# Head 2 turned by VectorE in tiles 1 to 6, and sums moved behind head 3's scores

## The chip, the core and the metric

The kernel runs on one core of a Trainium2 chip. The core has five engines that run their own instruction streams: TensorE (PE in the profile; its weight loads are PEld), VectorE (DVE), ScalarE (ACT), GpSimd (POOL) and SyncE (SP), which only issues transfers. Sixteen transfer (DMA) engines move data that SP and POOL ask for. The metric is the device time in microseconds (us) of one execution, as a median of runs; lower is better.

## The reference

The input x has 16 batches of 1024 nodes with 256 features; adj is a 1024 x 1024 matrix of 0 and 1 per batch. Two layers follow, each added to x:

```python
h = relu(layernorm(x))                          # layer 0
Q, K, V = h @ W.T + b, in 8 heads of 32         # Wq, Wk, Wv
s = where(adj == 0, -inf, Q @ K.T / sqrt(32))   # 1024 x 1024 for each head
x = x + (softmax(s) @ V, heads joined) @ Wo.T + bo

h = relu(layernorm(x))                          # layer 1
e = leaky_relu((h * a_0) @ h.T, 0.2)            # where adj == 1; other kinds have a_1 to a_3
x = x + softmax(where(adj == 1, e, -9e15)) @ h
```

The data has no kinds above 1, so a generic path at the kernel's end is skipped.

## The kernel before

A batch is cut into 8 tiles of 128 rows (t = 0 to 7), 128 tiles in all. The main loop goes over tiles s, and inside over the 8 heads h. Three stages overlap in it, all written out in one order by hand (`tc.manual_schedule()`), so each engine works off its instructions in program order:

- `now`: layer 0 of tile s (class `Attend`). `scores` (L461) puts a head's 128 x 1024 scores into one of two PSUM places (`sides`); heads 4 and 6 use side 1, the others side 0. `softmax_max` (L473, DVE) masks them and takes the maximum, writing the tile `p`; `softmax_exp` (L490, ACT) makes the exponentials, one head later.
- `was`: what is left of the tile before: the sums of heads 4 to 7 (`combine(1)`, L526, PE), their scaling (`combined`, L536, DVE), the output product (L541) and the residual (L547).
- `edge` and `edge_was`: layer 1 of the tiles 9 and 10 places earlier (class `Edges`). Its scores use side 1 (L633, L627), its maximum is L656, its own blocks come at h == 0, and `gather(0)` and `gather(1)` (L698, PE) multiply its probabilities with h, half of the columns each.

`piece` and `piece_was` project queries, keys and values of a batch that comes later.

The sums need each head's probabilities turned, with the keys along the partitions. There are two ways, two heads after the scores:

- `turn`: PE transposes eight 128 x 128 squares into PSUM (L590), and ACT copies them out in two halves (L591).
- `turn_blocks` and `place_blocks`: DVE transposes 32 x 32 blocks (L381), and SP issues four transfers of 128 KB (L386) that put the blocks in their places in the tile `pT`. The keys then come out in another order, which the values match for the heads in `MIXED`.

`by_blocks(t)` says which heads go the second way: 0, 1, 4 and 5 in tiles 1 to 6, 0, 1 and 4 in tile 7, 4 and 5 in tile 0. Layer 1's blocks go the second way in all tiles of the loop. Where a head's way doesn't fit its key order (`MIXED`), `softmax_exp` writes into a second tile `p` in the other order; before, that is heads 0 and 1 of tile 0 and head 5 of tile 7.

Around the change, the order in a tile is, at h == 3: scores of head 3, layer 1's maximum, head 3's maximum, exponential of head 2, layer 1's mirror copy (L647), value bias (L355), blocks of head 1, the next tile's query load (`load_queries`, L428, SP). At h == 4, with `late_scores`: exponential of head 3, `turn` of head 2, scores and maximum of head 4, and then `block()`: `combine(1)`, `combined`, `gather(0)`. At h == 7 come `gather(1)`, the store, and `combine(0)`, the sums of heads 0 to 3.

SP's queue in a tile, in order: layer 1's blocks, head 0's, head 1's, the query load, head 4's blocks, the write of x1 (L552), head 5's blocks, the store (L708).

Of the kernel before, what the change touches and what calls it, by code (L numbers as in the profile page):

```python
# [26 lines left out]
MIXED = (0, 1, 4, 5)  # L27
BY_BLOCKS = {7: (0, 1, 4), 0: (4, 5)}


def by_blocks(t):
    return BY_BLOCKS.get(t, MIXED)


def place_of(h):
# [12 lines left out]
def gnn_kernel(  # L48
# [308 lines left out]
    def load_key(b, h):  # L357
        kt = keys.tile([P, N], F32R, tag=f"k{h}", name=f"k{h}_{b}")
        c, r = divmod(h, GROUP)
        nc.sync.dma_start(  # L360
            out=kt.bitcast(F32),
            in_=kds[b][c, r * HD : (r + 1) * HD]
            .rearrange("d w n -> (d w) n").unsqueeze(1).to_broadcast([2 * HD, 2, N]),
        )
        keysets.setdefault(b, {})[h] = kt
# [410 lines left out]
    def attend_of(s):  # L776
        return Attend(*divmod(s, NT)) if 0 <= s < B * NT else None

    def edges_of(s):
        s -= LAG  # L780
        return Edges(*divmod(s, NT), s >= (B - 1) * NT) if 0 <= s < B * NT else None

    def piece_of(s):
        s += LEAD
        return Piece(*divmod(s, NT)) if s < B * NT else None

    with tc.manual_schedule():
        first = [Piece(0, 0, 4), Piece(0, 4, 4)]
        piece_was, piece_next = Piece(1, 0), piece_of(0)
        now, nxt = attend_of(0), attend_of(1)  # L790
# [48 lines left out]
        for s in range(B * NT + 1):  # L839
            b, t = divmod(s, NT)  # L840

            def load_keys(h, end):
                if t == NT - 1 and b + 1 < B and 2 * h + end in KEY_STEPS:
                    load_key(b + 1, KEY_STEPS.index(2 * h + end))
                if t == 0 and 0 < b < B and 2 * (HEADS + h) + end in KEY_STEPS:
                    load_key(b, KEY_STEPS.index(2 * (HEADS + h) + end))

            late_turn = None

            def block():  # L850
                if edge_was and not t:
                    edge_was.gather(0)
                if was:
                    was.combine(1)
                if not t and piece_was:
                    piece_was.biased()
                if was:
                    was.combined()
                if edge_was and t:
                    edge_was.gather(0)  # L860

            nxt2, edge_nxt, piece_nxt = attend_of(s + 2), edges_of(s + 1), piece_of(s + 1)
            for h in range(HEADS):
                ending, eh = (now, h - 1) if h >= 1 else (was, HEADS - 1)
                turning, th = (now, h - 2) if h >= 2 else (was, HEADS + h - 2)

                load_keys(h, 0)


                late_scores = h == 4 and now and 1 in by_blocks(t)  # L870
                if now and not late_scores:
                    now.scores(h)
                if h == 0 and piece_was:
                    piece_was.halve(0)
                if s == 0 and h == 1:
                    first[1].values()
                if h == 3 and edge:
                    edge.softmax_max()
                if h == 6:
                    if was:  # L880
                        was.residual()
                    norms(was, piece_nxt)
                if now and not late_scores:
                    now.softmax_max(h)
                if h == 4 and piece:
                    piece.normed()


                if h == 1 and edge:
                    edge.keep(0)  # L890
                if h == 2 and gone:
                    gone.turned_normed()
                if h == 5 and piece:
                    piece.turn()
                    piece.turned()
                if ending:
                    ending.softmax_exp(eh)

                if h == 3 and edge:
                    edge.keep(1)  # L900
                if h == 3 and was:
                    was.turned_reciprocals()
                if h == 3 and piece_was:
                    piece_was.raised(1)
                if h == 3 and edge:
                    edge.bend()


                if h == 3 and t and piece_was:
                    piece_was.biased()  # L910
                if h == 5 and was:
                    was.output()
                if h == 4 and not late_scores:
                    block()
                    late_turn = turning
                    load_keys(h, 1)
                    continue
                if h == 5 and late_turn:
                    late_turn.turn(2, 0)
                    late_turn.turn(2, 1)  # L920
                if h == 0 and t == 0 and was:
                    for half in range(2):
                        was.turn(HEADS - 3, half, nc.scalar.copy)
                if turning and th in by_blocks(turning.t):
                    turning.turn_blocks(th)
                    turning.place_blocks(th)
                elif turning and (h, t) != (HEADS - 1, NT - 1):
                    turning.turn(th, 0)
                    turning.turn(th, 1)
                if late_scores:  # L930
                    now.scores(h)
                    now.softmax_max(h)


                if h == 0:
                    if edge:
                        edge.score(0)
                    if gone:
                        gone.normed()
                    if edge_was:  # L940
                        edge_was.turn_blocks()
                        edge_was.place_blocks()
                if h == 1:
                    if gone:
                        gone.turn_normed()
                    if piece_was:
                        piece_was.project(1, 0)
                        piece_was.project(1, 1)
                    if was:
                        was.reciprocals()  # L950
                    if piece_nxt:
                        piece_nxt.load()
                if h == 2:
                    if edge:
                        edge.score(1)
                    if piece_was:
                        piece_was.values()
                    if was:
                        was.turn_reciprocals()
                        was.add_bias()  # L960
                if h == 3:
                    if nxt:
                        nxt.load_queries()
                    if edge:
                        edge.leak()
                    if piece_was:
                        piece_was.halve(1)
                    if edge_was:
                        edge_was.load_nodes()
                    if nxt:  # L970
                        nxt.flag()
                        nxt.mask()
                if h == 4:
                    block()
                if h == 5:
                    if piece_was:
                        piece_was.write_queries()
                    if edge_nxt:
                        edge_nxt.prepare()
                    if nxt2:  # L980
                        nxt2.load()
                if h == 6:
                    if piece:
                        piece.project(0, 0)
                        piece.project(0, 1)
                        piece.raised(0)
                    if edge:
                        edge.softmax_exp()
                    if was:
                        was.keep()  # L990
                    if now:
                        now.load_nodes()
                if h == 7:
                    if edge_was:
                        edge_was.gather(1)
                        edge_was.store()
                    if now:
                        now.combine(0)
                load_keys(h, 1)
            gone, was, now, nxt = was, now, nxt, nxt2  # L1000
            edge_was, edge = edge, edge_nxt
            piece_was, piece = piece, piece_nxt
# [84 lines left out]
```

## Time and profile before

| | |
|---|---|
| median of 3 runs | 3004.3 us (3004.06 to 3010.76) |
| the profiled execution's own time | 3006.89 us |
| its span, first to last instruction | 3005.0 us |
| granted TensorE clock | 0.998 |
| PE, DVE, ACT, POOL busy | 97%, 83%, 88%, 72% |
| mean DMA rate | 234 GB/s |

The busy share of PE is modelled from pipelined matmuls. In groups of instructions the columns after the count are the busy time in us, the mean of one in ns, and the idle time of the engine ahead of them with what ended it. Tiles are counted here from a tile's first softmax maximum to the next tile's.

### The profile page before, as it was taken

The numbers are of one execution on the slowest core, as the hardware profiler recorded it, in microseconds if no ns is written. First come the engines' busy times: TensorE is split into PE (matmuls) and PEld (weight loads), VectorE is DVE, ScalarE is ACT, GpSimd is POOL, SyncE is SP. The second block draws the span as 40 slices with busy tenths as digits, with TensorE's granted clock in tenths as the row PEclk, the third lists the DMA queues.
The fourth block names the chain that finished last, engine by engine and source line by source line (L and its number), as shares of the span: only waits on it lengthen the run. The fifth ranks groups of instructions, "written<-read, shape, count | busy, mean of one in ns | idle before, by whom it ended". The sixth has DMA issues, their size and how long they took to land. (4 is left out here: it accounts for less than half of the span.)

```text
span 3005.0 us, 95721 instructions
## 1 busy us (share of the span) xinstructions
PE 2903.3 (97%) x36594; PEld 2234.0 (74%) x36594; DVE 2495.4 (83%) x4405; ACT 2635.5 (88%) x5191; POOL 2171.0 (72%) x2999
## 2 busy tenths in 40 slices
PE   7889999999999999999999999999999999999998
PEld 5777777777777777777777777777777777777664
DVE  5888888888888888878888887888888888788875
ACT  5999989999898999999999998998989999898882
POOL 3767877777787777778778777777877777786542
PEclk9999999999999999999999999999999999999999
DMA  7787877778778887877878777787787878777763
GB/s 243 233 259 215 248 229 243 250 227 261 227 227 254 239 260 218 243 247 230 269 222 245 239 237 249 227 267 222 231 255 232 263 219 243 245 230 250 196 174 100
DMA packets 607041, 704.03 MB, mean 234 GB/s; under 512 B 64305, under 2 KB 537777, under 8 KB 606577
## 3 DMA queue, kind: packets, MB, share of 16 engines
q1 hardware_dynamic: 537504, 485.68, 54.4%
q0 software_dynamic: 66960, 210.04, 21.7%
q8 instruction: 294, 4.82, 0.7%
q10 hardware_dynamic: 2112, 2.10, 0.2%
q14 instruction: 171, 1.39, 0.1%
HBM read 252.98 MB, written 134.22 MB: 129 GB/s over the span
## 5 line engine op out<-in xcount | busy, mean ns | idle before, releaser
L473 DVE CUSTOM_DVE_ANT_0 p<-s,neg 128x1024 f32<-128x1024 f32 x1024 | 1238.6, 1210 | 344.8 <-PE s L461 324.6
L490 ACT ACTIVATE p<-p,nmx 128x1024 f32<-128x1024 f32 x1024 | 1236.4, 1214 | 51.6 <-DVE nmx L473 43.1
L461 PE MATMUL s<-k,qt 128*128 128x512 f32 x2048 | 743.2, 445 | 30.4 <-DMA k<-kd 8.3
L591 ACT COPY pT<-trp 128x512 f32<-128x512 f32 x1056 | 566.5, 593 | 77.5 <-PE trp L590 77.1
L590 PE MATMUL trp<-ident,p 128*128 128x128 f32 x4480 | 587.3, 274 | 27.4 <-ACT pT L591 15.0
L590 PEld LDWEIGHTS trp<-ident,p 128*128 128x128 f32 x4480 | 516.0, 140 | 118.9 <-ACT pT L591 30.2
L381 DVE STREAM_TRANSPOSE blocks<-p 128x1024 f32<-128x1024 f32 x472 | 585.2, 1240 | 11.1 <-ACT p L680 10.6
L526 PE MATMUL acc<-pT,v 128*32 128x128 f32 x16384 | 507.8, 273 | 9.3 <-ACT full L309 8.9
L526 PEld LDWEIGHTS acc<-pT,v 128*32 128x32 f32 x16384 | 453.4, 110 | 80.9 <-issue 36.1
L698 PE MATMUL acc<-h,pT 128*32 128x256 f32 x8192 | 510.0, 381 | 1.9 <-DMA pT<-blocks 1.6
L441 POOL TENSOR_SCALAR neg<-adj 128x1024 bf16<-128x1024 int32 x128 | 467.8, 3655 | 11.9 <-ACT neg L453 1.9
L676 POOL TENSOR_TENSOR sel<-sel,less 128x1024 f32<-128x1024 f32 x120 | 287.8, 2398 | 201.7 <-ACT less L665 201.7
L461 PEld LDWEIGHTS s<-k,qt 128*128 128x128 f32 x2048 | 312.4, 190 | 153.0 <-issue 82.5
L698 PEld LDWEIGHTS acc<-h,pT 128*32 128x32 f32 x8192 | 265.3, 110 | 190.7 <-issue 48.8
L633 PE MATMUL s<-h1T,ha 128*128 128x512 f32 (+2 forms) x744 | 272.8, 490 | 2.8 <-ACT h1T L569 2.8
L490 ACT ACTIVATION_READ_ACCUMULATOR p<-p,nmx 128x1 f32 x1024 | 213.3, 208 | 0.0
L330 POOL DMA_DIRECT2D kd<-halves x240 | 172.1, 766 | 35.5 <-POOL halves L314 35.4
L314 POOL TENSOR_TENSOR halves<-full,halves 128x256 fp32r<-128x256 f32 x240 | 176.5, 735 | 20.0
L674 POOL TENSOR_SCALAR less<-top 128x1 f32<-128x1 f32 x120 | 31.9, 266 | 213.0 <-DVE top L656 212.9
L647 ACT COPY mirror<-s 128x128 f32<-128x128 f32 (+3 forms) x208 | 76.1, 393 | 122.5 <-DVE top L656 102.9
L324 POOL DMA_DIRECT2D qd<-halves x240 | 177.8, 787 | 7.1
L633 PEld LDWEIGHTS s<-h1T,ha 128*128 128x128 f32 x744 | 126.7, 190 | 70.8 <-issue 44.8
(117 smaller groups left out, 4321.3 us busy)
## 6 DMA issues: line engine op xcount, KB each, us to landing
pT<-blocks SPq DMA_DIRECT2D x2368, 128.0 KB, 3.6
qt<-qd SPq DMA_DIRECT2D x128, 512.0 KB, 4.7
k<-kd SPq DMA_DIRECT2D x128, 512.0 KB, 6.8
adj<-in_adj POOLq DMA_DIRECT2D x127, 512.0 KB, 6.1
qd<-halves POOLq DMA_DIRECT2D x240, 256.0 KB, 4.0
kd<-halves POOLq DMA_DIRECT2D x240, 128.0 KB, 4.3
xb<-in_x POOLq DMA_DIRECT2D x128, 128.0 KB, 4.9
x1d<-x SPq DMA_DIRECT2D x128, 128.0 KB, 5.1
```

Of the source, the lines that this page charges most:

```text
L324: nc.gpsimd.dma_start(out=qds[self.b][self.first, oc].rearrange("p u w n -> p u (w n)"), in_=halves.unsqueeze(1).to_broadcast([P, 2, 2 * P]),)
L381: nc.vector.transpose(blocks.rearrange("p b j q -> p j b q"), p)
L441: nc.gpsimd.tensor_scalar(self.neg, self.adj, 0.0, MASKED, ALU.is_equal, ALU.mult)
L461: nc.tensor.matmul(self.ps[:, cols], lhsT=self.qt[:, h, :], rhs=keysets[self.b][h][:, cols], start=True, stop=True,)
L473: nc.vector.tensor_tensor_reduce(out=p, in0=sides[h in self.second], in1=self.neg, scale=-SCALE, scalar=FLOOR, op0=ALU.add, op1=ALU.min, a ...
L490: nc.scalar.activation(to, of, AF.Exp, bias=nmx, scale=-1.0, accum_out=self.sums[:, h : h + 1])
L526: nc.tensor.matmul(sums_place[r * HD : (r + 1) * HD, g * P : (g + 1) * P], lhsT=vs[self.b][:, j, place_of(h) : place_of(h) + HD], rhs=self ...
L590: nc.tensor.transpose(tr[:, j, :], p[:, jj * P : (jj + 1) * P], ident)
L591: copy(pT[:, half * 4 : half * 4 + 4, :], tr)
L633: nc.tensor.matmul(self.side[:, cols], lhsT=self.ha[:, c, :], rhs=h1T[:, c, cols], start=(c == 0), stop=(c == NC - 1),)
L676: nc.gpsimd.tensor_tensor(self.sel, self.sel, self.less, ALU.subtract)
L698: nc.tensor.matmul(self.sums[a * HD : (a + 1) * HD, :], lhsT=self.pT[:, j, a], rhs=h1s[self.b][:, j, :], start=(j == 0), stop=(j == NT - 1),)
```

## The change

In tiles 1 to 6 (`five`), head 2 joins the heads that DVE turns in blocks. As head 2 is not in `MIXED`, its exponential is written in another column order, into a second tile `p`. In these tiles `block()` stands right behind head 3 in PE's order, ahead of head 2's blocks and of head 4's scores. Head 0's blocks are made at the end of h == 1 instead of at h == 2; the value bias comes ahead of head 3's maximum; and the next tile's query load is issued at h == 5, behind head 2's blocks. Tiles 0 and 7 keep their order.

```diff
 def by_blocks(t):
-    return BY_BLOCKS.get(t, MIXED)
+    return BY_BLOCKS.get(t, (0, 1, 2, 4, 5))
...
+            five = now and 2 in by_blocks(t)
...
+                if h == 3 and five and piece_was:
+                    piece_was.biased()
...
-                if h == 3 and t and piece_was:
+                if h == 3 and t and not five and piece_was:
                     piece_was.biased()
...
-                if turning and th in by_blocks(turning.t):
+                if five and h == 4:
+                    block()
+                if turning is now and five and th == 0:
+                    pass
+                elif turning and th in by_blocks(turning.t):
                     turning.turn_blocks(th)
                     turning.place_blocks(th)
...
                     if was:
                         was.reciprocals()
+                    if five:
+                        now.turn_blocks(0)
+                        now.place_blocks(0)
...
                 if h == 3:
-                    if nxt:
+                    if nxt and not five:
                         nxt.load_queries()
...
-                if h == 4:
+                if h == 4 and not five:
                     block()
                 if h == 5:
+                    if nxt and five:
+                        nxt.load_queries()
```

## The prediction

> **What bounds the kernel now.** I read the page first (busy shares, costliest groups), then the busy time of six neighbouring tiles, then one of them in order of time, and last the transfer queue of SyncE (SP). The page:
>
> ```profile
> span 3005.0 us, 95721 instructions
> PE 2903.3 (97%) x36594; PEld 2234.0 (74%) x36594; DVE 2495.4 (83%) x4405; ACT 2635.5 (88%) x5191; POOL 2171.0 (72%) x2999
> ...
> L591 ACT COPY pT<-trp 128x512 f32<-128x512 f32 x1056 | 566.5, 593 | 77.5 <-PE trp L590 77.1
> L590 PE MATMUL trp<-ident,p 128*128 128x128 f32 x4480 | 587.3, 274 | 27.4 <-ACT pT L591 15.0
> ```
>
> TensorE (PE) is busy for 97%, and its transposes (L590) are 20% of that. The busy time of tiles 1 to 6 of batch 8, each from its first softmax maximum to that of the next tile (stretch, length, busy time of PE, PEld, DVE, ACT, POOL, clock, DMA share, GB/s):
>
> ```profile
> 1496.55:1519.52 22.97, 22.81 (x284) 16.99 (x283) 19.52 (x34) 20.78 (x43) 15.33 (x20) 1.00 0.72 203
> 1519.52:1542.16 22.64, 22.58 (x285) 17.21 (x284) 19.45 (x35) 20.61 (x42) 17.39 (x25) 1.00 0.77 227
> 1542.16:1564.50 22.34, 22.29 (x286) 17.30 (x285) 19.37 (x34) 20.39 (x41) 17.43 (x25) 1.00 0.78 232
> 1564.50:1586.59 22.09, 22.03 (x287) 17.17 (x286) 19.34 (x35) 20.17 (x40) 17.41 (x25) 1.00 0.80 233
> 1586.59:1608.55 21.96, 21.84 (x284) 16.80 (x283) 19.34 (x35) 20.06 (x40) 17.41 (x25) 1.00 0.80 235
> 1608.55:1630.39 21.84, 21.56 (x285) 16.85 (x284) 19.33 (x34) 19.95 (x40) 17.42 (x25) 1.00 0.80 237
> ```
>
> PE has no gap, the tile's length follows PE's, and VectorE (DVE) has 2.5 to 3.4 us free. Tile 3 on PE, in order of time, from head 3's scores to head 5's:
>
> ```profile
> 1549.46 0.71 PE L461 MATMUL s<-k,qt 128*128 128x512 f32 x2
> 1550.02 1.03 PE L590 MATMUL trp<-ident,p 128*128 128x128 f32 x8
> 1551.11 0.73 PE L461 MATMUL s<-k,qt 128*128 128x512 f32 x2
> 1551.77 1.95 PE L526 MATMUL acc<-pT,v 128*32 128x128 f32 x64
> 1553.54 1.91 PE L698 MATMUL acc<-h,pT 128*32 128x256 f32 x32
> 1555.38 0.73 PE L461 MATMUL s<-k,qt 128*128 128x512 f32 x2
> ```
>
> Head 2's eight transposes hold 1.09 us (1550.02 to 1551.11; the tail is head 4's scores waiting for ScalarE's mirror copy). The first sums (L698) begin at 1553.54. What they multiply comes by SP, whose issues around this tile are these, with the landing of the four from 1546.84 below:
>
> ```profile
> 1539.12 3.30 SPq L386 DMA_DIRECT2D pT<-blocks  x4
> 1542.47 0.60 SPq L552 DMA_DIRECT2D x1d<-x  x1
> 1543.19 2.81 SPq L386 DMA_DIRECT2D pT<-blocks  x4
> 1546.10 0.60 SPq L708 DMA_DIRECT2D out<-h  x1
> 1546.84 9.27 SPq L386 DMA_DIRECT2D pT<-blocks  x12
> 1556.22 0.54 SPq L428 DMA_DIRECT2D qt<-qd  x1
> 1561.45 2.89 SPq L386 DMA_DIRECT2D pT<-blocks  x4
> ```
> ```profile
> DMA to landing us min/median/max: 3.1/3.8/4.1
> ```
>
> The four at 1539.12 are head 4 of the tile before, those at 1543.19 head 5, the first four of the twelve layer 1's. SP issues without rest from head 4's blocks on, so layer 1's last block is issued at 1549.12 and lands at 1552.25: 13.1 us after 1539.12, and only 1.3 us before it is used. This is the second bound, just under the first.
>
> **The change part by part, in tiles 1 to 6 (96 of 128).**
>
> Removed from PE: head 2's slot, 1.09 us in tile 3; the same reading gives 0.79, 1.09, 1.09, 1.10, 0.99 and 1.19 for tiles 1 to 6, 1.04 on average. If PE alone counted, 96 x 1.04 = 100 us would go. It does not.
>
> Removed from ScalarE (ACT): two copies, 2 x 0.47 us from start to start. Added to ACT: head 2's exponential now writes in another column order. The nearest row is L490 in tiles 0 (heads 0, 1) and 7 (head 5), which writes at a step of 16 bytes:
>
> ```profile
> L490 ACT ACTIVATE p<-p,nmx x1024: 1136/1166/2304, 48.6 to 2917.6; 128x1024 f32<-128x1024 f32 x171
> ```
>
> Those take 2.16 to 2.30 us against 1.17. The new order steps by 128 bytes, which no row has. Ends: +0, because the mirror copies (L647) write at a 16-byte step from PSUM in 0.59 us, as L591's dense ones do; and +2.1, twice the row's excess. I take the row's +1.05, the same engine, size and memory. ACT's sum is then +0.1 per tile (ends -0.9 and +1.2), on 20.4 of 22.3 us.
>
> The skill against the trace: the Trainium skill, "SBUF — State Buffer", in its note on cachelines, says that accesses that keep moving to another 16-byte line pay a penalty, which speaks against this edit. Both the old step and the new one change line with every element, so by the page the new order costs about what the old one does, the sum above; the mirror copies show that it isn't paid everywhere.
>
> Added to DVE: one block transpose, 1.24 us (the same shape in L381), so 19.4 becomes 20.6 of 22.3 us. Added to SP and the transfer engines: four issues of about 0.7 us (2.89 for four) and 512 packets. Queue q1 spent 54.4% of the span on 537,504 packets, 3.0 ns each, so 1.6 us per tile: the DMA share goes from 0.78 to about 0.85. It falls at 13 to 16 us after the tile's start, where the queue has room.
>
> Moved on PE: combine(1) (heads 4 to 7) and gather(0) (layer 1's first sums) come directly behind head 3's scores, ahead of head 4's. Without a wait, gather would begin at 1549.46 + 0.65 + 1.77 = 1551.88; its last block lands at 1552.25. So the first sums now wait for SP's chain, and head 4's and 5's scores are queued behind them.
>
> Moved on DVE: the value bias ahead of head 3's maximum (its product ends at 1549.49, and DVE is free by then); head 0's blocks ahead of head 2's maximum, into an idle 0.90 us (it delays that maximum by some 0.3 us, and so head 2's exponential, the mirror and head 3's exponential by 0.4; PE's next use, head 3's transposes, has 0.3 us left). These cost nothing while PE waits for the sums. The transpose itself fits between the combined product and head 4's maximum, which has become later.
>
> Moved on SP: the query load goes behind eight block transfers instead of four. Head 1's blocks end about 10.3 us after the tile's start, eight issues take 5.2 to 5.8, so the load is issued at 15.6 to 16.2 (before: 14.06) and, with the 4.3 us that it takes here, lands at 20 to 20.5. The next scores need it at about 21.2. Head 2's blocks, last issued at about 15.2, land near 18 (2.6 us later, as head 1's), and the sums of heads 0 to 3 begin at 18.9 at the earliest. GpSimd's queue keeps its order; its mask and adjacency load come about 0.4 us later, behind ACT.
>
> The loop that this closes, in tile 3's rows: head 4's blocks issued to layer 1's last block landed, 13.25 (13.2, 13.1, 13.2, 13.6 and 13.1 in tiles 2 to 6); gather after its third of 32 products, for the fourth needs the last block, 1.84 x 29/32 = 1.67; head 4's scores to its maximum, 0.77 (as 1555.38 to 1556.15 for head 5); that maximum to the next, 1.13; head 5's maximum, residual and statistics to head 6's, 2.88; head 6's maximum and head 4's blocks to their issue, 2.42. Sum 22.12. Before, head 4's maximum lay ahead of gather and the same loop was 1.2 us shorter, so it never closed.
>
> So tiles 2 to 6 of a batch become 22.12 each, 110.6 against 22.64 + 22.34 + 22.09 + 21.96 + 21.84 = 110.87: -0.27. In tile 1, whose layer 1 blocks land early (behind tile 0's fewer blocks), head 5's maximum moves from 1511.29 to 1511.08 (scores 1504.92 + 0.65, combine 1.77, gather 1.84, then 0.77 + 1.13), and DVE, now without rest, saves the 0.2 us that it idles before the next tile: -0.4. Per batch -0.67; fourteen batches, -9.4. The last batch has no projections: its loop is 12.1 + 1.67 + 0.77 + 1.13 + 2.20 + 2.45 = 20.32 against 20.97, -0.65 in five tiles, -3. In batch 0 there is no layer 1; PE has 2.2 us free of 18.5, so I take 0 (ends -3 and +3). Sum -12 us of the profiled execution's 3006.9 (span 3005.0 and 1.9 around it). That one lay 2.6 us above the median of the three runs, so against 3004.3 I forecast 2992. No difference below 0.3% (9 us) can be told from none.
>
> **The rivals.**
>
> Slower, by one mechanism: the query load is late. Place: SP's queue, behind head 2's blocks. Against: 0.7 us of room by the above. For: it took 4.3 to 6.1 us in the tiles before, and now meets the blocks of head 4. If it takes 6, it lands at 21.9 and the next tile starts about 0.6 us later: 0.6 x 70 = +42, less the 12, about 3034. It decides from a landing 21.2 us after the tile's start. A dearer landing of layer 1's blocks acts in the same place: 13.73 was the mean in tiles 7, at a DMA share above 0.9, worth +0.4 x 70 = +28.
>
> The exponential is dearer than the row: at +2.1 ACT holds 21.6 us of a 22.2 us tile with all its waits, and I put the tile at 23: about +70, 3070. For: the wider step. Against: the row already pays for every element.
>
> PE's slot comes through: layer 1's blocks land 1 us earlier or the wait is shorter than I read. DVE's 20.6 us and 0.5 of waits then bound the tile at 21.1 to 21.3: -0.9 x 90 = -80, 2925. Against: gather already waited for these landings 38 times before (12.1 us).
>
> The change hides entirely: the loop and the old bound are equal to within 0.1 us per tile on average, within 9 us, around 3004.
>
> **How the numbers follow.** Loop as worked out, 2985 to 2995: 0.35. PE's slot largely through: 0.10. Hidden: 0.20. Late queries or later blocks: 0.23. Dear exponential: 0.12. So faster 0.45, same 0.20, slower 0.35. Alone, the likeliest has 2980 to 2995. The range leaves out most of the two far cases: 2965, which is the loop 0.4 us shorter (the blocks landing like the quickest tenth of the tiles), to 3045, the late queries with a little more.
>
> **What would show it.** Right: L698 waiting for the block transfers in nearly all tiles 2 to 6, some tens of us in all; L590's count 768 lower and L381's 96 higher; tiles 2 to 6 nearly equal at about 22.1, where they fell from 22.64 to 21.84; PE's busy time down by some 80 us with the span nearly the same; L490 with 144 long executions at about 2.2 us. Wrong: waits of L461 for the query load; an exponential of 3 us; tiles near 21.2; or tiles that still fall from 1 to 6, which would mean that PE and not the loop sets them.

## The result and the profile after

The changed kernel takes 3191.5 us (median of 4 runs, 3186.2 to 3193.8), the kernel before 3007.5 us beside it: a ratio of 1.0603, 95% interval 1.059 to 1.0616. The forecast was 2992 us with a range of 2965 to 3045, so it was wrong in sign and by far in size: +184 us in place of -12.

The page of the changed kernel (its groups: busy us, mean ns | idle us before, releaser and its part):

```profile
span 3188.8 us, 95035 instructions
PE 2891.2 (91%) x35826; PEld 2227.0 (70%) x35826; DVE 2595.6 (81%) x4501; ACT 2627.4 (82%) x4999; POOL 2168.7 (68%) x2999
...
L526 PE MATMUL acc<-pT,v 128*32 128x128 f32 x16384 | 572.3, 286 | 193.2 <-ACT recT L520 127.6
...
L590 PE MATMUL trp<-ident,p 128*128 128x128 f32 x3712 | 491.2, 276 | 19.6 <-ACT pT L591 15.8
```

The transposes went, as counted: L590 is 768 instructions and 96 us shorter. But PE's share fell from 97% to 91%, and a wait that had cost almost nothing now heads PE's list. From the waits of the changed kernel (us in total, times, longest):

```profile
PEld acc L526 <- ACT recT L520: 209.9, 97, 3.0
...
PE acc L526 <- ACT recT L520: 127.6, 73, 2.6
```

L526 are the sums of heads 4 to 7 (`combine(1)`), L520 is ScalarE's copy of the transposed reciprocals out of PSUM. It is one wait, seen by the weight load and by the matmul behind it (so the two are not added). 97 times is once in each of the 96 changed tiles and once more, 2.2 us on average; before, the same wait came once, for 0.4 us. PE's matmuls themselves stand for 168 us in the 96 tiles, 1.75 us each: for 23 of them (40 us) the profile names a block transfer, but in all 96 the first sum begins 0.05 us after L520's end. Tile 3 of batch 8, first PE, then ScalarE, in order of time:

```profile
1664.74 0.73 PE L461 MATMUL s<-k,qt 128*128 128x512 f32 x2
1667.65 2.05 PE L526 MATMUL acc<-pT,v 128*32 128x128 f32 x61 [2.19 <-ACT recT L520]
1669.44 0.38 PE L698 MATMUL acc<-h,pT 128*32 128x256 f32 x1
1669.50 0.31 PE L526 MATMUL acc<-pT,v 128*32 128x128 f32 x3
1669.61 1.93 PE L698 MATMUL acc<-h,pT 128*32 128x256 f32 x31
1671.47 1.21 PE L461 MATMUL s<-k,qt 128*128 128x512 f32 x4
```
```profile
1664.78 2.11 ACT L490 ACTIVATE p<-p,nmx 128x1024 f32<-128x1024 f32 x1 [2.03 <-DVE nmx L473]
1666.68 0.21 ACT L490 ACTIVATION_READ_ACCUMULATOR p<-p,nmx 128x1 f32 x1
1666.74 0.59 ACT L647 COPY mirror<-s 128x512 f32<-128x512 f32 x1
1667.21 0.40 ACT L520 COPY recT<-acc 128x256 f32<-128x256 f32 x1
```

PE is through with head 3's scores at 1665.5 and stands until 1667.65, when L520 has ended. L520 is queued behind head 2's exponential, which the change has made 1 us longer and which itself waits 2.03 us for head 2's maximum. The tile takes 23.95 us, of which PE is busy for 21.69. The six tiles of this batch (stretch, length, busy time of PE, PEld, DVE, ACT, POOL, clock, DMA share, GB/s):

```profile
1610.08:1634.15 24.07, 22.36 (x276) 16.47 (x275) 20.72 (x36) 20.74 (x41) 15.36 (x22) 1.00 0.74 214
1634.15:1657.31 23.16, 21.94 (x279) 16.85 (x278) 20.64 (x36) 20.55 (x40) 17.00 (x22) 1.00 0.80 239
1657.31:1681.26 23.95, 21.69 (x278) 16.77 (x277) 20.32 (x37) 20.32 (x39) 17.38 (x24) 1.00 0.81 240
1681.26:1705.01 23.75, 21.58 (x279) 16.66 (x278) 20.42 (x36) 20.09 (x38) 17.36 (x24) 1.00 0.82 239
1705.01:1728.08 23.07, 21.03 (x276) 16.25 (x275) 20.34 (x36) 20.00 (x38) 17.43 (x24) 1.00 0.84 245
1728.08:1751.06 22.98, 20.72 (x277) 16.30 (x276) 20.33 (x36) 19.86 (x38) 17.43 (x24) 1.00 0.84 247
```

No engine is full any more: a chain of waits sets the tile. Why does L526 wait for L520 at all? `combine(1)` writes `sums_place`, L520 reads `brief`, and these are two halves of one PSUM bank (`banks[0]`). The program makes PE wait for the readers of the whole bank; experiment 1, where the reciprocals have a place of their own, has no such wait. (The two halves are also one tile in the kernel; the runs don't tell which of the two the program goes by.) This agrees with the rule in the Trainium skill, "PSUM — Partial Sum Buffer", section "PSUM bank collisions raise a hardware error", that accesses of different engines are to be kept apart by bank and quadrant, not by address; here the wait between the halves is the 209.9 us above.

A part of the price could have been worked out from the trace of before. There, in the same tile, ScalarE ran head 2's exponential and L520 so:

```profile
1548.25 1.15 ACT L490 ACTIVATE p<-p,nmx 128x1024 f32<-128x1024 f32 x1 [0.46 <-DVE nmx L473]
1550.47 0.59 ACT L647 COPY mirror<-s 128x512 f32<-128x512 f32 x1 [0.97 <-DVE top L656]
1550.95 0.38 ACT L520 COPY recT<-acc 128x256 f32<-128x256 f32 x1
```

L520 ended at 1551.33, and the sums began at 1551.77, so head 2's transposes and head 4's scores covered it. The forecast had them begin at 1549.46 + 0.65 = 1550.11, so these rows give a wait of 1.22 us. The exponential's extra 1.05 us does not simply add to that: ScalarE stood 0.97 us between it and the mirror copy, waiting for layer 1's maximum, and this idle time would have taken up nearly all of it. The rest of the wait comes from a later start, behind which the longer exponential does count. Head 2's exponential began 1.21 us ahead of head 3's scores (1549.46) before, and begins 0.04 us behind them (1664.74) now, since head 2's maximum stands behind head 0's blocks, and those waited for their buffer:

```profile
1662.31 1.25 DVE L381 STREAM_TRANSPOSE blocks<-p 128x1024 f32<-128x1024 f32 x1 [1.19 <-DMA pT<-blocks]
1663.48 1.19 DVE L473 CUSTOM_DVE_ANT_0 p<-s,neg 128x1024 f32<-128x1024 f32 x1
```

In the mean of tiles 1 to 6 of batches 1 to 14, the exponential began 1.23 us ahead of head 3's scores and begins 0.43 us ahead of them now; it took 1.15 us and takes 2.13; and L520 ended 1.80 us after the start of these scores and ends 2.35 us after it now. Late start and longer exponential together have used up the idle time ahead of the mirror copy (0.98 us on average before, none now) and moved L520 back by 0.55 us.

In tile 3, from the start of head 3's scores to the end of the first sums, the kernel before needs 5.92 us, head 4's scores included. In the changed one head 4's scores begin 6.73 us after head 3's, and with their 0.66 us it is 7.39: +1.47 us in this tile, where the move without a wait would have given -1.09.

The clock is lower too. The mean granted clock is 0.981 against 0.998: 0.019 x 3188.8 - 0.002 x 3005.0 = 55 us of PE's full speed lost, 20 of them in batch 0, 27 in batches 1 to 14 and 7 after them. In tile 4 of batch 2 (the same columns):

```profile
538.50:539.00 0.50, 0.08 (x1) 0.08 (x2) 0.50 (x3) 0.50 (x3) 0.00 (x0) 1.00 0.70 213
539.00:539.50 0.50, 0.50 (x14) 0.46 (x18) 0.50 (x1) 0.50 (x3) 0.00 (x0) 0.86 0.69 205
539.50:540.00 0.50, 0.50 (x17) 0.50 (x12) 0.25 (x1) 0.50 (x1) 0.00 (x0) 0.50 0.75 219
...
542.50:543.00 0.50, 0.50 (x13) 0.29 (x8) 0.27 (x1) 0.50 (x2) 0.50 (x2) 0.72 0.72 186
```

After 2.16 us of waiting PE gets half of its clock from about 539.4 to 542.8, and the tile takes 25.6 us. The tile above, with a wait of 2.19 us, kept its full clock.

By place, from the first softmax maximum of each batch: batch 0 grew by 43.8 us (155.9 to 199.7), batches 1 to 14 by 127.2, the last one and the end by 12.6. With 0.2 us ahead of batch 0 that is the 183.8 us by which the span grew.

### The profile page after: what moved, and what is told of

Read it like the earlier page. It is cut to its first block, busy times and chain, and to the rows that moved or that the text cites. A ratio compares the mean times of both kernels' runs of the same rounds, so it can differ in the third digit from the quotient of the medians.

```text
span 3188.8 us, 95035 instructions
## 1 busy us (share of the span) xinstructions
PE 2891.2 (91%) x35826; PEld 2227.0 (70%) x35826; DVE 2595.6 (81%) x4501; ACT 2627.4 (82%) x4999; POOL 2168.7 (68%) x2999
## 5 line engine op out<-in xcount | busy, mean ns | idle before, releaser
L490 ACT ACTIVATE p<-p,nmx 128x1024 f32<-128x1024 f32 x1024 | 1326.3, 1299 | 175.9 <-DVE nmx L473 169.0
L461 PE MATMUL s<-k,qt 128*128 128x512 f32 x2048 | 722.7, 442 | 47.6 <-DVE nmx L473 21.1
L381 DVE STREAM_TRANSPOSE blocks<-p 128x1024 f32<-128x1024 f32 x568 | 704.5, 1240 | 58.7 <-DMA pT<-blocks 33.9
L526 PE MATMUL acc<-pT,v 128*32 128x128 f32 x16384 | 572.3, 286 | 193.2 <-ACT recT L520 127.6
L526 PEld LDWEIGHTS acc<-pT,v 128*32 128x32 f32 x16384 | 506.7, 115 | 278.8 <-ACT recT L520 209.9
L591 ACT COPY pT<-trp 128x512 f32<-128x512 f32 x864 | 461.7, 588 | 114.2 <-PE trp L590 114.1
L698 PE MATMUL acc<-h,pT 128*32 128x256 f32 x8192 | 532.2, 384 | 2.2 <-DMA pT<-blocks 1.8
L590 PE MATMUL trp<-ident,p 128*128 128x128 f32 x3712 | 491.2, 276 | 19.6 <-ACT pT L591 15.8
L590 PEld LDWEIGHTS trp<-ident,p 128*128 128x128 f32 x3712 | 430.6, 141 | 96.2 <-ACT pT L591 30.8
L441 POOL TENSOR_SCALAR neg<-adj 128x1024 bf16<-128x1024 int32 x128 | 467.7, 3654 | 11.9 <-ACT neg L453 1.8
L698 PEld LDWEIGHTS acc<-h,pT 128*32 128x32 f32 x8192 | 300.2, 111 | 179.8 <-issue 51.1
L674 POOL TENSOR_SCALAR less<-top 128x1 f32<-128x1 f32 x120 | 31.8, 265 | 260.1 <-DVE top L656 260.1
L536 DVE TENSOR_TENSOR recT<-acc,recT 128x256 f32<-128x256 f32 x128 | 54.2, 423 | 167.4 <-PE acc L526 167.3
L510 POOL COPY wide<-rec 128x256 f32<-128x256 f32 x128 | 59.5, 465 | 190.4 <-DVE rec L508 182.9
```

Source lines behind the costliest of these rows:

```text
L381: nc.vector.transpose(blocks.rearrange("p b j q -> p j b q"), p)
L441: nc.gpsimd.tensor_scalar(self.neg, self.adj, 0.0, MASKED, ALU.is_equal, ALU.mult)
L461: nc.tensor.matmul(self.ps[:, cols], lhsT=self.qt[:, h, :], rhs=keysets[self.b][h][:, cols], start=True, stop=True,)
L490: nc.scalar.activation(to, of, AF.Exp, bias=nmx, scale=-1.0, accum_out=self.sums[:, h : h + 1])
L526: nc.tensor.matmul(sums_place[r * HD : (r + 1) * HD, g * P : (g + 1) * P], lhsT=vs[self.b][:, j, place_of(h) : place_of(h) + HD], rhs=self ...
L590: nc.tensor.transpose(tr[:, j, :], p[:, jj * P : (jj + 1) * P], ident)
```

## The experiments

Each ratio is to the kernel before on the same chip; "interval" is 95%. Waits are of the profiled execution.

**1, the bank alone.** The changed kernel, with the transposed reciprocals in a place of head transposes, not in `brief`:

```diff
-            self.rec_ps = by_chunk(brief)
+            self.rec_ps = ps_tr.tile([P, 4, P], F32, tag="tr", name="trr")[:, :NC]
```

> The changed kernel, with the transposed reciprocals (L516) put into a PSUM place of the transposes instead of the half bank beside the sums. Theory A (heads 4 to 7's sums stand in the same PSUM bank as the reciprocals' transpose, so behind head 3's scores they wait until ScalarE has copied it, L520, which stands behind head 2's exponential): the wait of L526 for L520 (210 us) goes, tiles 2 to 6 come to about 22.2 us and the kernel to 3000 to 3030. Theory B (the added block transfers and SP's queue are what is late): still above 3150. Theory C (head 2's dearer exponential fills ScalarE): still above 3120.

3129.6 us, ratio 1.0398 (1.0378 to 1.0418). The wait L526 <- L520 is gone, the clock is back at 0.995, but only 62 of the 184 us are: 31 of them in batch 0, 15 after batch 14, and no more than 15 in batches 1 to 14. So the bank is a part of the cause there, not the whole that theory A took it for. Two other waits came up:

```profile
DVE blocks L381 <- DMA pT<-blocks: 118.5, 68, 3.1
...
PEld acc L698 <- ACT full L309: 65.0, 62, 1.2
```

The first: head 0's blocks, moved earlier, now need the buffer that head 4's blocks of the tile before still hold while they are sent. The second: layer 1's first sums use `early`, the place from which ScalarE reads the projected queries (L309), right behind L520.

**2, the exponential alone.** The changed kernel with head 2's exponential written densely (its sums then take keys and values that do not belong together):

```diff
-            if (h in MIXED) != (h in by_blocks(self.t)):
+            if h != 2 and (h in MIXED) != (h in by_blocks(self.t)):
```

> The changed kernel, but head 2's exponential keeps its column order and is written densely in place, so that head 2's probabilities meet the values in the wrong order (this part of the result is changed). Theory A: the copy L520 comes 1.0 us earlier per tile, so the tiles shorten by about that, 96 x 1.0 to 1.3 us with fewer spells of the lower clock: 3060 to 3100. Theory B: above 3160. Theory C: 3020 or less.

3133.0 us, ratio 1.0406 (1.0385 to 1.0427), in none of the three ranges expected: 58 us less, 0.61 us for each of 96 tiles, and the wait on PEld falls from 209.9 to 142.7 us. The dense exponential also takes no second tile `p`, but it begins as before the edit, 0.41 us ahead of head 3's scores on average (0.43); only its length changes, 1.15 us for 2.13. So the strided order is on the path here, in front of L520.

**3, the order alone.** The kernel before with `block()` and the value bias moved as in the change, head 2 still on PE:

```diff
+                moved = now and 1 <= t <= 6
+                if moved and h == 4:
+                    block()
...
-                if h == 4:
+                if h == 4 and not moved:
                     block()
```

> The kernel before, with only the sums and products (and the value bias) moved behind head 3's scores in tiles 1 to 6; head 2 is still turned on TensorE, behind them. Theory A: the wait for L520 is there without any new transfer or dearer exponential; L520's result stands at 9.2 us after the tile's start, then 1.8 + 1.8 + 0.8 + 0.8 us to head 4's maximum, 1.5 us later than now for head 5's: 3080 to 3150. Theories B and C: no loss, 3020 or less.

3125.4 us, ratio 1.0381 (1.036 to 1.0402): 115 us of loss with no block transpose, no transfer and no strided exponential added.

```profile
PEld acc L526 <- ACT recT L520: 158.2, 97, 2.6
```

The arithmetic above gives a wait of 1551.33 - 1550.11 = 1.22 us, and 0.65 + 1.22 + 1.77 + 1.84 + 0.66 + 1.04 (head 2's transposes, now behind the sums) - 5.92 = +1.26 per tile, 121 us in 96 tiles. PE's matmuls stood for 1.21 us in each of the 96, 116 us, and again each first sum began 0.05 us after L520's end. The clock has no part in this: it was 0.996.

**4, the turn alone.** The kernel before with `by_blocks` changed and nothing moved:

```diff
-    return BY_BLOCKS.get(t, MIXED)
+    return BY_BLOCKS.get(t, (0, 1, 2, 4, 5))
```

> The kernel before, with only head 2 turned by VectorE in tiles 1 to 6; the sums stay behind head 4's scores, head 0's blocks and the query load stay where they were. Theory A: only the mirror copy and with it head 4's scores come 0.3 to 0.4 us later, no wait for L520: 3000 to 3050. Theory B: 3150 or more. Theory C: 3100 or more.

3302.4 us, ratio 1.0969 (1.0947 to 1.0991), the worst of all, where theory A had 3000 to 3050:

```profile
PEld s L461 <- ACT mirror L647: 202.5, 105, 3.2
...
ACT p L490 <- DVE blocks L381: 136.0, 96, 1.7
```

Head 2's exponential needs a second tile `p`, and the buffer it gets is one that head 0's blocks still read; the mirror copy, and with it head 4's scores, then come late. So with the blocks of head 0 where they were, the turn costs more than the whole change. The turn with head 0's blocks moved, but the sums left in their place, was not run.

**5 to 8: more pieces freed.** 5 is experiment 1 with the query copy (L309) ahead of head 2's exponential; 7 is the changed kernel with layer 1's blocks in the buffer of `less`; 6 is both; 8 is 6 with the dense exponential of experiment 2. The edit of the query copy, then that of the buffer:

```diff
+                if h == 3 and five and piece_was:
+                    piece_was.raised(1)
                 if ending:
                     ending.softmax_exp(eh)
...
-                if h == 3 and piece_was:
+                if h == 3 and not five and piece_was:
                     piece_was.raised(1)
```
```diff
         def turn_blocks(self):
-            self.blocks = blocks_of(self.sel)
+            if self.last:
+                self.blocks = blocks_of(self.sel)
+            else:
+                place = work.tile([P, N], F32, tag="less", name="eblocks", bufs=1)
...
```

> The changed kernel with the reciprocals in a place of the transposes, as in the run before, and the copy of the query projection (L309), which reads the bank that layer 1's first sums write, ahead of head 2's exponential on ScalarE. Theory A2 (both PSUM banks hold the sums back): the wait of L698 for L309 (113 us in the run before) goes, 60 to 80 us less than there: 3050 to 3070. Theory D (head 0's blocks, now earlier, wait for the buffer that head 4's transfers are still reading, and set the time): no gain over 3130, and L381 waits for transfers at least as long as there (118 us). Theory E (head 2's blocks land too late for the sums of heads 0 to 3): no gain over 3130, L526 waits for transfers.

> The run above, and layer 1's blocks in a buffer of their own (that of its slope term), so that the three block buffers serve layer 0 alone. Theory A2 alone: as the run above. Theory D: L381's wait for transfers goes and 60 to 100 us with it: 2980 to 3030. Theory E: 3080 or more, with L526 waiting for transfers.

> The changed kernel with only layer 1's blocks in a buffer of their own. Theory A2: the sums still wait for ScalarE, at most L381's 34 us of waits go: 3150 to 3190. Theory D: 3100 or less.

> Both banks and the buffer as above, and head 2's exponential written densely in the old column order (head 2's probabilities meet the values in the wrong order, this part of the result is changed). If ScalarE is then still on the path, 1.0 us per tile goes, some 60 to 90 us against the run with the sparse exponential; if the loop through SyncE's transfers (22.1 us per tile) is the bound, no more than 20 us, and the time is 2980 to 3010.

| | us | ratio (interval) |
|---|---|---|
| 5, both banks | 3145.2 | 1.0452 (1.0422 to 1.0482) |
| 6, banks and buffer | 3141.3 | 1.0439 (1.0383 to 1.0495) |
| 7, buffer alone | 3154.8 | 1.0484 (1.0454 to 1.0514) |
| 8, as 6, dense exponential | 3138.8 | 1.0431 (1.04 to 1.0461) |

The buffer alone is worth 37 us, with a new wait of its own (77.4 us of ScalarE's L665 for that buffer): head 0's blocks no longer wait, and head 2's exponential begins 0.84 us ahead of head 3's scores on average. The earlier query copy (5 against 1) gained nothing, since the copy itself waited, in front of the exponential (for what, stands at 16). In 6 this wait is the first line below, and a wait from the forecast is the second, layer 1's first sums for layer 1's blocks:

```profile
ACT full L309 <- POOL less L674: 88.2, 42, 2.6
...
PEld acc L704 <- DMA pT<-eblocks: 61.9, 159, 2.4
```

6 and 8 do not differ in time. In batches 1 to 14 the dense one is 17 us shorter, and in batch 0, at half clock for longer, 16 us longer; so with the first bank free, little of the exponential's 1 us per tile is on the path.

**9 and 10: SP's order.** 9 is experiment 6 with the x1 write (L552) and the store (L708) issued behind layer 1's blocks; 10 adds the query load ahead of head 2's blocks, as before the change.

```diff
+                    if gone:
+                        gone.keep()
+                    if edge_gone:
+                        edge_gone.send()
...
-                    if was:
-                        was.keep()
...
-                        edge_was.store()
+                        edge_was.store(send=False)
```
```diff
-                    if nxt and not five:
+                    if nxt:
                         nxt.load_queries()
...
-                    if nxt and five:
-                        nxt.load_queries()
```

> Both banks and the buffer as before, and on SyncE the write of x1 and the store of the result are issued behind layer 1's blocks instead of ahead of them: two issues, 1.4 us, fewer in the chain from head 4's blocks to layer 1's last landing. Loop theory (with both banks free, the tile is that chain, 14.4 us, plus 8.9 us from the landing to the next tile's head 4 blocks): 1.2 to 1.4 us per tile in 75 tiles, 90 to 100 us less than there: 3035 to 3055. Rival F (the next bound is as near: query load at 21.7 us, or head 2's blocks for the sums of heads 0 to 3): under 30 us gained.

> The run above with the query load ahead of head 2's blocks on SyncE. Loop theory: no more than 20 us from it. Rival F with the query load as the next bound: another 40 us or more; with head 2's blocks as the next bound: slower than the run above by 20 us or more.

9 takes 3094.6 us (1.0287, 1.0263 to 1.0311), 47 less than 6, between the two ranges expected. 10 takes 3136.1 (1.0425, 1.0401 to 1.0449): the queries land 3.2 us earlier (18.2 us after the tile's start), but head 2's blocks come behind them and the sums of heads 0 to 3 wait for blocks 47.6 us (9.2 in 9). One of the two transfers is late in either order.

**11, SP's order in the kernel before.** The edit of 9 on the kernel before.

> The kernel before, with only the write of x1 and the store issued behind layer 1's blocks. There the chain has 0.9 us of room, so by the loop theory nothing changes but tile 7 and a few tiles that wait for a late landing: 0 to 12 us less than before, 2995 to 3010.

2998.6 us (6 runs), 0.9967 (0.9954 to 0.9979): a little faster than the kernel before.

**12 and 13: no shared bank at all.** 12 is experiment 9 with ScalarE's order as in the changed kernel, and the query projection in a place of the transposes too; 13 is 12 with the dense exponential.

```diff
+            elif which == 1:
+                if oc == 0:
+                    self.q_ps = ps_tr.tile([P, 4, P], F32, tag="tr", name="trq")
+                ps = self.q_ps[:, oc, :]
```

> The changed kernel with nothing of the wait chain left that the runs so far have shown: the transposed reciprocals and the query projection both take places of the transposes (so neither of the two sum banks is shared with a piece that ScalarE reads late), ScalarE's order is the changed kernel's own, layer 1's blocks have a buffer of their own, and SyncE issues the x1 write and the store behind layer 1's blocks. Theory A, the loop of the prediction holds once it is free: landing part 13.2 us plus the tail of 8.9 us, so tiles 2 to 6 of about 22.1 us and 3000 to 3030 us in all. Theory B, the next bound is the query load and head 2's blocks, which land at 21 to 22 us and 19 to 20 us of the tile: tiles stay at 22.8 to 23.2 us and the time at 3060 to 3100 us.

> The run before this one with head 2's exponential written densely, in the wrong key order, so that the sums of head 2 take keys and values that do not belong together; the work is otherwise the same, and ScalarE has 1.0 us per tile less to do. If ScalarE's dearer exponential is still on the path: 40 to 95 us less than that run (0.4 to 1.0 us in 96 tiles). If the transfers bound the tile: within 10 us of it.

3133.4 us (1.0407, 1.039 to 1.0425) and 3158.7 (1.0489, 1.0468 to 1.051). Both lie above the ranges expected. The borrowed place costs elsewhere: the projection waits for the copies of the transposes (98.7 us on PE), and tiles 0 (27.9 us, 25.8 in the changed kernel) and 7 (24.0, 22.3) are longer. 17 below, which differs from 12 in this place alone, is 77 us faster. In tiles 1 to 6 (batches 1 to 14) both take the same, 22.92 and 22.94 us, so the exponential is not on the path here. Of the 25 us by which 13 is slower, 20 lie in batch 0, where the clock was lower; by the clock, 0.989 against 0.998, 0.011 x 3157 - 0.002 x 3131 = 28 us of PE's full speed went. Why it fell more in 13 stays open.

**14, an earlier layer 1 maximum in the kernel before.** Experiment 11, with head 0's blocks behind head 3's maximum in tiles with layer 1.

```diff
+                if h == 3 and now and edge and 0 in by_blocks(t):
+                    now.turn_blocks(0)
+                    now.place_blocks(0)
...
+                swap = now and edge and 0 in by_blocks(t)
+                if h == 2 and swap:
+                    pass
```

> The kernel before with the x1 write and the store behind layer 1's blocks (2998.6 us), and head 0's blocks on VectorE behind head 3's maximum, so that layer 1's maximum, the mirror copy and the exponential of head 3 come up to 1.2 us earlier and TensorE waits less for the mirror copy ahead of head 4's scores. Theory A, that wait of about 0.3 us per tile goes: 10 to 30 us less, 2970 to 2990 us. Theory B, TensorE only waits elsewhere, or the query load, which stands behind head 0's blocks in SyncE's queue, lands after the next scores need it: 2995 to 3030 us.

2988.8 us, 0.9933 (0.9916 to 0.9949), faster than both kernels and a little faster than 11. PE's small wait for the mirror copy (30.9 us before) falls to 1.2 us, and the tiles that nothing disturbs follow PE's busy time again, shorter than before (22.09 and 21.84 us in tiles 4 and 6 of the same batch; the mean of tiles 1 to 6 in batches 1 to 14 is 22.14 against 22.31):

```profile
1556.77:1578.34 21.57, 21.57 (x287) 17.19 (x286) 19.33 (x34) 20.14 (x40) 16.17 (x22) 1.00 0.75 228
...
1600.20:1621.43 21.23, 21.10 (x285) 16.92 (x284) 19.33 (x34) 19.94 (x40) 17.25 (x25) 1.00 0.82 243
```

**15 to 18: the split between the order and the turn.** 15 is the order alone (3) with the reciprocals' own place; 16 is the order alone with all of 9; 17 is 9 without the earlier query copy; 18 is 15 with SP's order of 9.

> The order alone (sums of heads 4 to 7 and layer 1's first sums behind head 3's scores, head 2 still on TensorE), which took 3125.4 us, with the transposed reciprocals in a place of the transposes. Theory A, the shared bank is the whole price of the order: 3000 to 3030 us. Theory B, it is about the half of it, and the query projection, which shares the other sum bank with layer 1's sums and is read by ScalarE behind head 2's exponential, holds the first sums next: 3050 to 3080 us, with waits of the first sums for the query copies of some 100 us.

> The order alone with all that the run of 3094.6 us has (both sum banks free early, layer 1's blocks in their own buffer, the x1 write and the store behind layer 1's blocks), but head 2 turned on TensorE as before, so without the 384 added transfers, the added block transpose and the dearer exponential. Theory A, the order costs nothing once its banks are free, and what is left of the loss at 3094.6 us is the turn itself: 2985 to 3020 us. Theory B, the order itself costs most of what is left, whoever turns head 2: 3060 to 3095 us.

> The run of 3094.6 us with ScalarE's order as in the changed kernel, that is, without my earlier copy of the query projection, which made things worse in the run of the order with all free: so own place for the reciprocals, own buffer for layer 1's blocks, x1 write and store behind layer 1's blocks. Theory A, the earlier copy cost more than its bank was worth: 3040 to 3075 us. Theory B, the second shared bank takes it back, with waits of layer 1's first sums for the query copies of 100 us or more: 3090 to 3130 us.

> The order alone with its own place for the reciprocals (3064.3 us), and the x1 write and the store behind layer 1's blocks. There the first sums waited 50 us for layer 1's blocks, so if that loop bounds it, the time falls by 20 to 45 us, to 3020 to 3045 us; if TensorE's other waits bound it, 3055 to 3070 us. The difference between this run and the other one of this call is the price of turning head 2 on VectorE in the best state that I found: by the loop of the prediction 0 to 15 us, by dearer landings 20 to 50 us.

| | us | ratio (interval) |
|---|---|---|
| 15, order, own bank | 3064.3 | 1.0169 (1.015 to 1.0189) |
| 16, order, all of 9 | 3153.0 | 1.0468 (1.0451 to 1.0486) |
| 17, order and turn, bank, buffer, SP's order | 3056.6 | 1.0156 (1.0137 to 1.0175) |
| 18, order, bank, SP's order | 3019.7 | 1.003 (1.0019 to 1.004) |

16 shows what the earlier query copy cost, and lies outside both ranges expected, since neither theory had the copy's own wait:

```profile
ACT full L309 <- POOL less L674: 248.4, 83, 3.1
...
PEld trh L237 <- ACT pT L591: 188.7, 103, 3.0
```

The profile names GpSimd's L674, but that only ends at about the same time. In this kernel the copy stands in front of L674 in the program, and what it reads (`early`) shares the bank `banks[1]` with what VectorE's value bias, L355, reads (`late`). In 16, as in 5, 6, 9 and 10, the copy waited in 90 tiles, and in 89 of them it began within 0.2 us of L355's end (0.12 as a rule):

```profile
1511.68 0.42 DVE L355 TENSOR_TENSOR v<-acc,bv_t 128x256 f32<-128x256 f32 x1
1512.21 0.63 ACT L309 ACTIVATE full<-acc,bq_t 128x128 f32<-128x128 f32 x2 [3.06 <-POOL less L674]
```

So by the trace the copy waits for L355, which stands behind layer 1's maximum on VectorE; that the shared bank is the reason is likely, but was not tried.

Taken out, 17 is 38 us faster than 9. In the order alone, the shared bank was 61 of the 115 us (3 to 15). Of the rest of 15, layer 1's first sums wait 50.3 us for layer 1's blocks, as the loop of the forecast has it; the 100 us of waits for the query copies that theory B expected are 1.6. SP's order takes another 45 us (15 to 18): the order is then 9 us above the kernel before, though against the kernel before with the same SP order (11) it still costs some 20. The turn of head 2 by VectorE, with all that it brings along (its exponential's order, head 0's blocks, the query load), costs 37 us in this cleanest state (18 to 17; 17 also has the buffer, which in the changed kernel was a gain), and 66 in the changed kernel (3 to after). Its waits in 17, against 0.9 us and 2.2 us for the same two lines in 18:

```profile
PE acc L526 <- DMA pT<-blocks: 48.1, 62, 2.3
...
PE s L461 <- DMA qt<-qd: 19.6, 33, 1.6
```

These are the sums of heads 0 to 3 waiting for head 2's blocks (40.6 of the 48.1 us), and the next tile's scores waiting for the queries.

## Why the prediction was wrong

**What bounds the kernel (right).** PE did; the counts of L590 and L381 came out as stated. PE's busy time fell by 12 us, half-rate work included, and by 45 in 17; 80 had been forecast. PE's slot did not come through, as forecast, but for another reason.

**"Moved on PE" (the step that failed).** The prediction let the sums of heads 4 to 7 begin 0.65 us after head 3's scores and looked for a wait only in the first sums behind them. It checked what the sums multiply, but not where they write: the bank, and with it L520 in ScalarE's queue. By the rows of before the missed term is 1.22 us per tile, and worked out it makes the order alone +121 us; that measured +115, with 1.21 us of PE's time in each of 96 tiles. (With the bank freed 61 of them went, in 15; then layer 1's blocks came next.) In the changed kernel the wait is 1.75 us per tile, 168 us. The prediction's rivals named late queries, late blocks and a dear exponential; none named ScalarE's queue in front of the sums.

**"Removed and added on ACT".** The price was right: the new order takes 2.08 to 2.17 us, +0.97 against the +1.05 taken. Its place was wrong. It was set against ScalarE's sum per tile, but it stands in front of L520, and cost 58 us there (2). Where L520 no longer held the sums, it cost nothing (13 against 12) or little (8 against 6).

**"Moved on DVE … cost nothing" (wrong).** Head 0's blocks did not find "an idle 0.90 us" only, but also a buffer still being sent: 33.9 us of waits in the changed kernel, 118.5 once the first bank was free, and 37 us of time in experiment 7. Head 2's exponential was to come 0.4 us later; against head 3's scores it comes 0.80 us later, and 0.39 where the buffer is free (7). This delay, too, stands in front of L520. The buffers' number (three) and the transfers that hold them were not looked at. With head 0's blocks left where they were, on the other hand, the second tile `p` is late (4).

**"The loop" (its parts nearly right, not what bound the changed kernel).** In tiles 2 to 6 it was worked out as 13.25 us from head 4's blocks to the landing of layer 1's last, and 8.87 from there to the next head 4's blocks. In the trace of the changed kernel these are 12.8 and 11.0 on average in batches 1 to 14: the blocks landed in time, at 10.0 us of the tile, and the first sums began at 11.9, held by the bank. The stated sign of being right, L698 waiting for transfers in nearly all tiles, did not appear there (13.6 us in 39 times on both parts of PE). With the banks freed it did, in 6: the tail then was 8.95, nearly as worked out, but the landing part 14.4. In 17 the parts are 13.5 and 9.1, 22.6 in all, against the 22.12 forecast. So the tail's sum holds, and the landing was taken 0.2 to 1.1 us too short, being read from a trace with fewer transfers.

**"Moved on SP" (0.7 us of room was not there).** The query load was issued at 17.1 us of the tile and landed at 21.8 (forecast 15.6 to 16.2, and 20 to 20.5). The landing took 4.7 us, near the 4.3 taken; the issue was late, as VectorE's head 2 blocks stand behind the combined product, and that behind the delayed sums. In batch 0 the queries were late by up to 3.0 us. That was the rival given 3034 us; in 17, where it is not hidden by longer tiles, it shows as the 19.6 us above.

**Batch 0 (taken at nothing, ends -3 and +3).** It cost 43.8 us, a quarter of the loss. The order alone did not lengthen it (155.8 against 155.9 us), the turn alone did (212.1, experiment 4), the bank's own place gave 31 of the changed kernel's loss back (169.0), and its tiles ran at a granted clock of 0.81 to 0.98. PE's free 2.2 us, which the forecast counted as a cushion, may be what lets the clock fall there under a further wait; that was only argued, not tried.

**What remains open.** The order alone is 115 of the 184 us and shown. The 66 us from there to the changed kernel are not split: the longer exponential (58, experiment 2), the buffer (37, experiment 7), the late transfers and the clock's 55 us of PE's full speed overlap, and how much of each would stay without the others was not tried. Nor were the 37 us of the turn split between VectorE's block transpose and the 384 added transfers.

## What to carry to other kernels

When work is moved ahead on an engine, look at the place it writes as well as at what it reads: who else uses that PSUM bank or buffer, on which engine that user is queued, and when it ended in the old trace. That one row (L520's end at 1551.33) would have given the 1.22 us per tile that the order alone costs. A dearer instruction on an engine with time to spare is not free if something short that others wait for stands behind it in that engine's queue.

## What the runs showed of the hardware

After only 2.16 us without work PE's clock fell to half for about 3.4 us, in one tile and not in another with the same gap. The Trainium skill, "TensorE: Matmul & The Clock Gate", Part 1, gives a free-running window of about 3.4 us and warns of gaps longer than that; the length of the spell agrees, but here shorter gaps were enough, and the measurement decides. Gaps of 1.5 to 2.6 us between PE's matmuls came 75 times in the changed kernel and 3 times before, at mean clocks of 0.981 and 0.998. The changed kernel has 31 spells at half clock, and in the 3.4 us ahead of each PE was idle for 1.6 to 3.1 us; most of the 75 gaps were followed by none.

An fp32 exponential from SBUF to SBUF takes 2.08 to 2.17 us when it writes at a step of 128 bytes, and 2.13 to 2.25 in tile 0 at 16 bytes, against 1.15 dense: the wider step is no dearer than the narrow one.
